# Projecting the scan outputs of two channel groups together in a state-space layer

## The chip, the cores and the metric

The kernel runs on one core of a Trainium2 chip. The metric is the device time of one execution in microseconds (us); lower is better. The core has a matrix engine (TensorE, PE in the profile; its weight loads are listed as PEld), three engines for element-wise work (VectorE or DVE, ScalarE or ACT, GpSimd or POOL) and a queue processor (SyncE or SP) that here only issues DMAs. Each engine takes its instructions in program order; engines meet through semaphores. On-chip data lie in SBUF, with 128 partitions (rows), and matrix products land in PSUM, which has eight banks of 128 x 512 float32.

## The reference

One layer of a convolutional network with a mixture of experts behind it, for 4 images of 256 channels and 32 x 32 = 1024 positions, in float32. The change concerns its first piece. The 256 normalised channels are split into 4 groups of 64 channels (NB = 4, DM = 64), and each group runs its own selective scan with 128 inner channels (DIN) and 16 states (DS):

```python
def selective_scan(u, dt, Bm, Cm, A, Dp):
    dA = jnp.exp(dt[..., None] * A)
    dBu = (dt * u)[..., None] * Bm[:, :, None, :]
    def step(h, inp):
        dA_t, dBu_t, C_t = inp
        h = dA_t * h + dBu_t
        return (h, jnp.einsum('bds,bs->bd', h, C_t))
    ...
    return ys.transpose(1, 0, 2) + u * Dp

def mamba(xs, inw, convw, convb, xpw, dtw, dtb, alog, dp, outw):
    xz = xs @ inw.T
    u, z = jnp.split(xz, 2, axis=-1)
    ...
    y = selective_scan(u, dt, Bm, Cm, -jnp.exp(alog), dp)
    return y * jax.nn.silu(z) @ outw.T
...
xc = xn.reshape(B, N, NB, DM).transpose(2, 0, 1, 3)
xm = mamba_v(xc, m_inw, m_convw, m_convb, m_xpw, m_dtw, m_dtb, m_alog, m_d, m_outw) + skip_scale * xc
```

The last factor of each group's output is the gate `silu(z)`, then comes the output projection from 128 inner channels to the group's 64 channels, and the normalised input scaled by `skip_scale` is added. Behind `xm` come one-dimensional convolutions, an eight-headed attention over the 1024 positions, a feed-forward product, a depthwise 3 x 3 convolution with normalisations, and at the end the experts (8 of them, two per position).

## The kernel before, in words

**Layout.** Channels lie on partitions, positions along the free axis. The 256 channels of an image are two blocks of 128 rows; `where(n)` gives for group n the block `c = n // 2` and its 64 rows `rows` within it. So groups 0 and 1 are the two halves of block 0, groups 2 and 3 those of block 1. Positions are treated in two halves h of 512 (HALF), one PSUM bank each.

**Parts and steps.** One image b, one group n and one half h make a part; `parts` lists all 32 of them, n before h, b outermost. A part has 16 scan steps. A step makes, for 32 inner channels and 4 states on 128 rows, the decay `exp(dt A)` on ACT (L718, `decay`, issued three steps ahead: LEAD = 3), the inflow `dt u B` on VectorE (L728), the scan itself on VectorE (L739) and the product with C on POOL (L747). TensorE spreads B over the rows (L710, `spread_b`) and sums the states into the PSUM tile `yp` (L757, `sums_of`).

**Order.** The whole stage is one hand-written order (`tc.manual_schedule`): `scan` (L833) emits, at each of the 16 steps, what the dictionaries `before`, `behind` and `group` name for that step. `before` finishes the previous part while the current one scans: at step 1 the last state sums, at step 3 `gather`, at step 6 `project_out`, at step 8 `add_skip`. So the output of part k is projected during part k+1. At the last part before an image's attention (the second half of group 1 in images 1 to 3), and at the very last part, `finish_part` (L868) does these things at once.

**The work that the change touches.** `gather` (L762) copies `yp` from PSUM to an SBUF tile `y` on ACT (L764) and multiplies it in place with the gate `z` on POOL (L765). `project_out` (L767) forms the group's output in a PSUM tile `op`: first the skip, a 64 x 64 diagonal product of the normalised input (L770), then the projection from 128 rows to the group's 64 rows added on top (L774). In float32 each of these matrix products shows as two records. `add_skip` (L776) copies the 64 rows on ACT into `XM[b]` (L780), the padded image that the convolutions read. `XM[b]` is taken from its pool when group 0's first half arrives. `z` is one tile for both halves of a group, filled by `copy_z` (L637) and passed through silu while the group before it scans.

**Beside the scan.** While image b scans, image b-1's later work is spread between its steps: `convolutions(b - 1)` from the start of image b, with diagonal products L426 and full 128 x 128 products L428 on TensorE, and after the fourth part the scan is halted for `attention(b - 1)` (L1117, L1137, L1163); then come `joined`, `local`, `around` and `sent_off`. `raw` (L1794) and its copy `XR` (L1786) lie in the last of these. What remains of image 3 and the experts comes after the last part.

**Buffers.** Tiles come from rotating pools: `act8` (8 buffers of 2 x 1024, where XM lies), `act4` (7 of 1024: z, u and others), `act2` (16 of 512: the decays, the scan outputs, y and others) and `psum` (8 banks, with op, yp, the B products and much of the work beside the scan). A tile whose buffer is still being read waits for that reader.

Of the kernel before, what the change touches and what calls it, by code (L numbers as in the profile page):

```python
# [9 lines left out]
F32 = mybir.dt.float32  # L10
AF = mybir.ActivationFunctionType
ALU = mybir.AluOpType
AX = mybir.AxisListType

P = 128
# [3 lines left out]
N = HH * WW  # L19
HALF = 512  # L20
NB, DM, DIN, DS, DTR, KC = 4, 64, 128, 16, 4, 4
# [3 lines left out]
LEFT = KC - 1  # L25
# [50 lines left out]
def network(  # L76
# [27 lines left out]
    nc = tc.nc  # L104
# [18 lines left out]
    def col(name, i=0, rows=slice(0, P)):  # L123
        at = _AT[name] + i
        return V[rows, at : at + 1]

    ident = cpool.tile([P, P], F32, name="ident")
# [19 lines left out]

    with tc.tile_pool(name="w_conv", bufs=1) as wp, tc.tile_pool(
        name="act8", bufs=8
    ) as act8, tc.tile_pool(name="act4", bufs=7) as act4, tc.tile_pool(  # L150
        name="act2", bufs=16
    ) as act2, tc.tile_pool(name="steps", bufs=2) as actd, tc.tile_pool(
        name="steps4", bufs=6
    ) as acts, tc.tile_pool(name="rows", bufs=3) as actc, tc.tile_pool(
        name="small", bufs=1
    ) as small, tc.tile_pool(
        name="spread", bufs=4, space=bass.MemoryType.DRAM
    ) as spread:

        XN = {}  # L160
# [10 lines left out]
        def load(ap, name, eng=None):  # L171
            t = wp.tile(list(ap.shape), F32, name=name)
            if eng is None:
                later.append((t, ap))
            else:
                eng.dma_start(t, ap)
            return t
# [10 lines left out]
        moutT_s = load(moutT, "moutT_s", nc.gpsimd)  # L188
# [135 lines left out]
        nc.vector.tensor_reduce(quads, ident.rearrange("p (s g) -> p g s", s=4), AX.X, ALU.add)  # L324
        A = wp.tile([P, GD, NB, GS], F32, name="A")
        inwk = wp.tile([P, NB, 2, DIN], F32, name="inwk")
        skips = wp.tile([P, DM], F32, name="skips")
        keeps = wp.tile([P, NB, P], F32, name="keeps")
        wdt = wp.tile([P, NB, DIN], F32, name="wdt")
        al = act4.tile([P, GD, NB * DS], F32, tag="a4", name="al")  # L330
# [6 lines left out]
        def weights():  # L337


            for n in range(NB):  # L340
                diag = a2(f"diag_{n}").rearrange("p (k d) -> p k d", k=KC)
                at = _AT["convw"] + n * KC
                nc.vector.tensor_tensor(
                    diag, ident.rearrange("p (a d) -> p a d", a=1).to_broadcast([P, KC, P]),
                    V[:, at : at + KC].rearrange("p (k a) -> p k a", a=1).to_broadcast([P, KC, P]),
                    ALU.mult,
                )
                taps = ps(f"taps_{n}")
                nc.tensor.matmul(
                    taps, ones, diag.rearrange("p k d -> p (k d)"), start=True, stop=True  # L350
                )
                yield 1
                for i in range(2):
                    r = ts(i, DM)
                    nc.vector.tensor_tensor(
                        inwk[r, n], taps[r].rearrange("p (k d) -> p k d", k=KC)[:, ts(i, 2), :],
                        inuT_s[r, n].rearrange("p (a d) -> p a d", a=1).to_broadcast([DM, 2, DIN]),
                        ALU.mult,
                    )

            for n in range(NB):
                xp = ps(f"xpw_{n}")
                nc.tensor.transpose(xp[0:DTR, 0:P], xpwT_s[:, n, 0:DTR], ident)
                xpw = a2(f"xpw_s_{n}", DTR)
                nc.scalar.copy(xpw[:, 0:P], xp[0:DTR, 0:P])
                yield 1
                wd = ps(f"wd_{n}")
                nc.tensor.matmul(wd[:, 0:P], xpw[:, 0:P], dtw_s[:, n, :], start=True, stop=True)
                nc.scalar.copy(wdt[:, n, :], wd[:, 0:P])
            for i, r in enumerate(states):  # L370
                nc.scalar.activation(
                    A[r].rearrange("p g n s -> p (g n s)"),
                    al[r].rearrange("p g c -> p (g c)")
                    .rearrange("p (x s) -> p x s", s=4)[:, :, i : i + 1]
                    .rearrange("p x s -> p (x s)"),
                    AF.Exp,
                )
            yield 1
            nc.vector.tensor_scalar(A, A, -1.0, None, ALU.mult)
            nc.vector.tensor_reduce(  # L380
                skips, ident.rearrange("p (s g) -> p g s", s=2), AX.X, ALU.add
            )
            nc.vector.tensor_scalar(skips, skips, col("skip"), None, ALU.mult)
            for n in range(NB):
                nc.vector.tensor_scalar(keeps[:, n, :], ident, col("dskip", n), None, ALU.mult)

        def ps(name):

            return psum.tile([P, HALF], F32, tag="ps", name=name)
# [4 lines left out]
        def a8_padded(name):  # L394
            t = act8.tile([P, NC2, N + 2], F32, tag="a8", name=name)
            nc.gpsimd.memset(t[:, :, 0:1], 0.0)
            nc.gpsimd.memset(t[:, :, N + 1 : N + 2], 0.0)
            return t

        def a4(name):  # L400
            return act4.tile([P, N], F32, tag="a4", name=name)

        def a2(name, rows=P):
            return act2.tile([rows, HALF], F32, tag="a2", name=name)

        def half(h):
            return ts(h, HALF)
# [81 lines left out]
        XM = {}  # L489
# [105 lines left out]
        T = {}  # L595
# [3 lines left out]
        def where(n):  # L599
            return n // 2, slice((n % 2) * DM, (n % 2) * DM + DM)  # L600
# [159 lines left out]
                )  # L760

        def gather(b, n, h):  # L762
            y = T[b, n, h, "y"] = a2(f"y_{b}_{n}_{h}")
            nc.scalar.copy(y, T[b, n, h, "yp"])  # L764
            nc.gpsimd.tensor_tensor(y, y, T[b, n, "z"][:, half(h)], ALU.mult)  # L765

        def project_out(b, n, h):  # L767
            c, rows = where(n)
            op = T[b, n, h, "op"] = ps(f"op_{b}_{n}_{h}")
            nc.tensor.matmul(  # L770
                op[rows], skips[rows], XN[b][rows, c, ds(LEFT + h * HALF, HALF)],
                start=True, stop=False,
            )
            nc.tensor.matmul(op[rows], moutT_s[:, n, :], T[b, n, h, "y"], start=False, stop=True)  # L774

        def add_skip(b, n, h):  # L776
            c, rows = where(n)
            if n == 0 and h == 0:
                XM[b] = a8_padded(f"xm_{b}")
            nc.scalar.copy(XM[b][rows, c, ds(1 + h * HALF, HALF)], T[b, n, h, "op"][rows])  # L780


        before = {
            1: [(sums_of, GS - 1)], 3: [(gather,)], 6: [(project_out,)], 8: [(add_skip,)],
        }

# [240 lines left out]

        def largest(b, g, q, k):

            each = small.tile([P, 4, N // P, 2], F32, tag="each", name=f"each_{b}_{g}")  # L1030
            for i in range(4):
                r = ts(i, HD)
                for qt in range(N // P):
                    for h in range(2):
                        sp = ps(f"sp_{b}_{g}_{i}_{qt}_{h}")
                        nc.tensor.matmul(
                            sp, q[r, ts(qt, P)], k[r, half(h)], start=True, stop=True
                        )
                        nc.vector.tensor_reduce(
                            each[:, i, qt, h : h + 1], sp, AX.X, ALU.max, negate=True  # L1040
                        )
            mneg = small.tile([P, 4 * N // P, 1], F32, tag="mneg", name=f"mneg_{b}_{g}")
            nc.vector.tensor_reduce(
                mneg, each.rearrange("p i t h -> p (i t) h"), AX.X, ALU.min
            )
            tp = ps(f"mT_{b}_{g}")
            nc.tensor.transpose(tp[0 : 4 * N // P, 0:P], mneg.rearrange("p i a -> p (i a)"), ident)
            mT = small.tile([4 * N // P, P], F32, tag="mT", name=f"mT_{b}_{g}")
            nc.scalar.copy(mT, tp[0 : 4 * N // P, 0:P])
            rows = a4(f"mrow_{b}_{g}")  # L1050
            for i in range(4):
                nc.sync.dma_start(
                    rows[HD * i : HD * i + 1, :].rearrange("a (t x) -> a t x", x=P),
                    mT[ts(i, N // P), :],
                )
            return rows
# [41 lines left out]
        def attention(b):  # L1098
# [4 lines left out]
            v8, qk = QKV.pop(b)  # L1103
            rows = [
                largest(b, g, qk[g][:, 0, :], qk[g][:, 1, :]) if shifted else None
                for g in range(2)
            ]
# [426 lines left out]
        with tc.manual_schedule(engines=ALL):  # L1534
            log_exp()
            start(weights(), first_normalised())
            drain()
            first_part()
            for b in range(B):
                for p in range(PARTS):  # L1540
                    at = b * PARTS + p
                    stop = b > 0 and p == PARTS // 2 - 1 or at == len(parts) - 1
# [72 lines left out]
class Experts:  # L1615
# [11 lines left out]
    T = 256  # L1627
# [798 lines left out]
```

## Time and profile before

| What | us |
|---|---|
| Three executions | 2192.04, 2197.09, 2203.86 |
| Median | 2197.09 |
| The profiled execution | 2216.93 |
| Its span, first to last instruction | 2215.0 |
| TensorE busy in it | 1975.0 |
| VectorE busy | 1534.4 |
| ACT busy | 1222.4 |
| POOL busy | 1047.5 |
| Mean granted TensorE clock | 0.947 of full speed |

All shares and instants are from the profiled execution. Its timeline falls into stages: image 0's scan alone until about 297 us; then, for each of images 1 to 3, four parts of scan with the convolutions of the image before (the last of these parts ends at about 440, 800 and 1202 us), that image's attention (until 536, 897 and 1298 us), and four more parts of scan. The last scan part ends at about 1460 us, and the rest of image 3 and the experts fill the time to 2215.

In the lines of the profile an instruction is named by its line in the kernel, its engine, its operation and its tiles (output <- inputs) with partitions x elements. A number in square brackets at the end of a timeline line is the time its engine stood idle before it, with what ended that.

### The profile page before, as it was taken

Reading aid. Unit: us, or ns where it says so; the run is one execution under the profiler, and the core shown is the slowest. Engines: PE = TensorE matmul, PEld = TensorE weight load, DVE = VectorE, ACT = ScalarE, POOL = GpSimd, SP = SyncE. Lnnn points to the kernel's source line nnn. Section 1 sums busy time; section 2 is a strip of 40 time slices with the busy share of each in tenths; the row PEclk is TensorE's granted clock in tenths of the full one; section 3 lists DMA queues with packets and bytes.
Section 4 is the critical chain, followed back from the end, with each engine's and each line's share of the span. In section 5 each row is a group of like instructions: output and inputs, shape, how many; then the busy total and the mean of one; then the engine's idle time right before and its main releaser. Section 6 shows DMA issues by size and latency. Waiting matters only on the chain. (4 is left out here: it accounts for less than half of the span.)

```text
span 2215.0 us, 28220 instructions
## 1 busy us (share of the span) xinstructions
PE 1975.0 (89%) x8722; PEld 879.7 (40%) x8722; DVE 1534.4 (69%) x2232; ACT 1222.4 (55%) x2288; POOL 1047.5 (47%) x930
## 2 busy tenths in 40 slices
PE   6878879999987999986889999678999989999995
PEld 2113112322212332322223223135732668888884
DVE  3999999858999978799798978984255355211211
ACT  4665657678767667675656765543248433222221
POOL 0787888612788740576975025741130012422221
PEclk8898999999999999998999999889989999999997
DMA  3664553401544421244533034353320166966665
GB/s 95 151 165 118 125 133 83 114 9 59 123 116 105 106 49 39 59 117 104 160 94 92 1 91 106 86 178 113 101 89 1 46 193 175 271 176 187 178 167 164
DMA packets 157088, 251.41 MB, mean 114 GB/s; under 512 B 34740, under 2 KB 101332, under 8 KB 156664
## 3 DMA queue, kind: packets, MB, share of 16 engines
q1 hardware_dynamic: 136560, 223.47, 36.3%
q0 software_dynamic: 12720, 17.32, 3.9%
q10 hardware_dynamic: 7640, 8.65, 1.2%
q8 instruction: 72, 1.18, 0.2%
q14 instruction: 96, 0.79, 0.1%
HBM read 137.22 MB, written 36.62 MB: 78 GB/s over the span
## 5 line engine op out<-in xcount | busy, mean ns | idle before, releaser
L747 POOL TENSOR_TENSOR dA<-hs,cs 128x512 f32<-128x512 f32 x512 | 682.2, 1342 | 388.5 <-DVE hs L739 268.9
L718 ACT ACTIVATE dA<-dts,A 128x512 f32<-128x512 f32 x512 | 358.8, 718 | 143.5 <-DMA dts<-dt 72.4
L2293 POOL DMA_INDIRECT Y<-ys,dest x68 | 108.9, 1601 | 528.3 <-DVE ys L2285 521.2
L757 PE MATMUL yp<-dA,quads 128*32 128x512 f32 x1024 | 272.2, 632 | 71.2 <-POOL dA L747 60.9
L1127 ACT ACTIVATE e<-st 128x512 f32<-128x512 f32 x512 | 263.7, 604 | 111.3 <-PE st L1117 89.3
L728 DVE TENSOR_TENSOR dBu<-dts,bs 128x512 f32<-128x512 f32 x384 | 259.9, 678 | 56.6 <-PE bs L710 18.1
L2258 ACT ACTIVATE hs<-h,b 128x256 f32<-128x256 f32 (+1 forms) x256 | 110.2, 479 | 339.6 <-PE h L2253 224.1
L2266 PE MATMUL y<-w,hs 128*128 128x256 f32 (+1 forms) x1088 | 245.7, 385 | 1.9 <-ACT hs L2258 1.9
L739 DVE TENSOR_TENSOR_SCAN hs<-dA,last,dBu 128x512 f32<-128x512 f32 x192 | 243.6, 1269 | 4.4 <-PE yp L757 1.3
L2253 PE MATMUL h<-xT,w 128*128 128x256 f32 (+1 forms) x1024 | 238.6, 389 | 0.2 <-DVE xT L2216 0.2
L739 DVE TENSOR_TENSOR_SCAN hs<-dA,dBu 128x512 f32<-128x512 f32 x192 | 231.8, 1207 | 9.6 <-PE av L1137 6.5
L1173 DVE TENSOR_TENSOR e<-e,e 128x512 f32<-128x512 f32 x256 | 170.3, 726 | 90.2 <-ACT e L1127 40.3
L2266 PEld LDWEIGHTS y<-w,hs 128*128 128x128 f32 (+1 forms) x1088 | 199.0, 190 | 39.2 <-issue 8.9
L2253 PEld LDWEIGHTS h<-xT,w 128*128 128x128 f32 x1024 | 195.2, 192 | 44.4 <-issue 11.0
L2216 DVE COPY xT<-xp 128x512 f32<-128x512 f32 (+1 forms) x36 | 23.3, 646 | 243.7 <-PE xp L2212 243.4
L710 PE MATMUL bs<-u,xpwT_s 128*32 128x512 f32 x1024 | 160.8, 660 | 34.7 <-DVE hs L739 14.4
L1117 PE MATMUL st<-qk 32*128 32x512 f32 x1024 | 182.0, 645 | 7.0 <-ACT e L1127 3.0
L757 PEld LDWEIGHTS yp<-dA,quads 128*32 128x32 f32 x1024 | 49.3, 113 | 270.1 <-POOL dA L747 169.6
L1163 PE MATMUL av<-e,v 128*32 128x512 f32 x1024 | 141.9, 618 | 0.0
L1117 PEld LDWEIGHTS st<-qk 32*128 32x128 f32 x1024 | 61.5, 184 | 126.3 <-issue 91.4
L1137 PE MATMUL av<-e,every 128*32 128x512 f32 x512 | 90.3, 623 | 3.1 <-DVE e L1173 3.0
L728 DVE TENSOR_TENSOR bs<-dts,bs 128x512 f32<-128x512 f32 x128 | 86.1, 673 | 1.3 <-DMA dts<-dt 1.3
(336 smaller groups left out, 2678.3 us busy)
## 6 DMA issues: line engine op xcount, KB each, us to landing
dts<-dt SPq DMA_DIRECT2D x512, 128.0 KB
w<-in_W_dram SPq DMA_DIRECT2D x124, 512.0 KB
cs<-cd SPq DMA_DIRECT2D x512, 64.0 KB
xs<-XS SPq DMA_DIRECT2D x32, 260.0 KB
xd<-xn SPq DMA_DIRECT2D x64, 128.0 KB
xn<-in_x_dram SPq DMA_DIRECT2D x8, 512.0 KB
XL<-xl SPq DMA_DIRECT2D x8, 512.0 KB
xl<-XL SPq DMA_DIRECT2D x4, 1024.0 KB
```

The source lines that it names most:

```text
L710: nc.tensor.matmul(bs[r], xpwT_s[:, n, s : s + 1].to_broadcast([P, 32]), T[b, n, "u"][:, half(h)], start=True, stop=True,)
L718: nc.scalar.activation(dA, T[b, n, h, "dts", g][:, 0, :], AF.Exp, scale=A[:, g, n, q : q + 1])
L728: nc.vector.tensor_tensor(dBu, T[b, n, h, "dts", g][:, 1, :], T[b, n, h, "bs", q], ALU.mult)
L739: nc.vector.tensor_tensor_scan(hs, T[b, n, h, "dA", i], dBu, 0.0 if h == 0 else last, ALU.mult, ALU.add)
L747: nc.gpsimd.tensor_tensor(dA, hs, T[b, n, h, "cs", q], ALU.mult)
L757: nc.tensor.matmul(T[b, n, h, "yp"][ts(g, 32)], quads, T[b, n, h, "dA", q * GD + g], start=False, stop=(q == GS - 1),)
L1117: nc.tensor.matmul(sts[i], k[r, ts(kt, P)], q[r, half(h)], start=True, stop=not shifted)
L1127: nc.scalar.activation(es[i], sts[i], AF.Exp, scale=1.0 / HD**0.5)
L1163: nc.tensor.matmul(accs[0][ts(i, HD)], v8[:, kt, ts(4 * g + i, HD)], es[i], start=(kt == 0), stop=(kt == NK - 1),)
L1173: nc.vector.tensor_tensor(first[i], first[i], es[i], ALU.add)
L2253: nc.tensor.matmul(hp[:, i, :], w1(c, k0 + i), xT[:, c, :], start=(c == 0), stop=(c == NC2 - 1))
L2266: nc.tensor.matmul(yp[ts(k % parts, n), ts(t % 2, C)], hidden(k)[:, ds(t * P, n)], w2(k), start=(k < parts), stop=(k >= NHC - parts),)
```

## The change

Groups 0 and 1 (and 2 and 3) share a block of 128 rows. The changed kernel leaves an even group's gated output where it is and projects it together with that of the odd group after it.

- `gather` writes the gated output into the gate's own tile `z`, and `y` is only read by that product.
- `project_out` and `add_skip` do nothing for even n. For odd n, `project_out` makes one skip product over all 128 rows of the block and then two projections, of the even group into rows 0 to 63 and of the odd one into rows 64 to 127 of the same PSUM tile; `add_skip` copies 128 rows.
- `XM[b]` is taken at group 1's first half, two parts later.
- `skips` becomes a 128 x 128 diagonal.
- The pool `act4` has eight buffers.
- Three small tiles in `largest`, which belongs to a second network that is not executed in these runs, are taken from `act2`.

```diff
-    ) as act8, tc.tile_pool(name="act4", bufs=7) as act4, tc.tile_pool(
+    ) as act8, tc.tile_pool(name="act4", bufs=8) as act4, tc.tile_pool(
...
-        skips = wp.tile([P, DM], F32, name="skips")
+        skips = wp.tile([P, P], F32, name="skips")
...
-            nc.vector.tensor_reduce(
-                skips, ident.rearrange("p (s g) -> p g s", s=2), AX.X, ALU.add
-            )
-            nc.vector.tensor_scalar(skips, skips, col("skip"), None, ALU.mult)
+            nc.vector.tensor_scalar(skips, ident, col("skip"), None, ALU.mult)
...
         def gather(b, n, h):
-            y = T[b, n, h, "y"] = a2(f"y_{b}_{n}_{h}")
+            y, z = a2(f"y_{b}_{n}_{h}"), T[b, n, "z"][:, half(h)]
             nc.scalar.copy(y, T[b, n, h, "yp"])
-            nc.gpsimd.tensor_tensor(y, y, T[b, n, "z"][:, half(h)], ALU.mult)
+            nc.gpsimd.tensor_tensor(z, y, z, ALU.mult)

         def project_out(b, n, h):
             c, rows = where(n)
-            op = T[b, n, h, "op"] = ps(f"op_{b}_{n}_{h}")
+            if n % 2 == 0:
+                return
+            op = T[b, c, h, "op"] = ps(f"op_{b}_{c}_{h}")
             nc.tensor.matmul(
-                op[rows], skips[rows], XN[b][rows, c, ds(LEFT + h * HALF, HALF)],
-                start=True, stop=False,
-            )
-            nc.tensor.matmul(op[rows], moutT_s[:, n, :], T[b, n, h, "y"], start=False, stop=True)
+                op, skips, XN[b][:, c, ds(LEFT + h * HALF, HALF)], start=True, stop=False
+            )
+            for i in range(2):
+                nc.tensor.matmul(
+                    op[ts(i, DM)], moutT_s[:, 2 * c + i, :],
+                    T[b, 2 * c + i, "z"][:, half(h)], start=False, stop=True,
+                )

         def add_skip(b, n, h):
             c, rows = where(n)
-            if n == 0 and h == 0:
+            if n % 2 == 0:
+                return
+            if n == 1 and h == 0:
                 XM[b] = a8_padded(f"xm_{b}")
-            nc.scalar.copy(XM[b][rows, c, ds(1 + h * HALF, HALF)], T[b, n, h, "op"][rows])
+            nc.scalar.copy(XM[b][:, c, ds(1 + h * HALF, HALF)], T[b, c, h, "op"])
...
-            each = small.tile([P, 4, N // P, 2], F32, tag="each", name=f"each_{b}_{g}")
+            each = a2(f"each_{b}_{g}")[:, 0 : 8 * N // P].rearrange(
+                "p (i t h) -> p i t h", i=4, h=2
+            )
...
-            mneg = small.tile([P, 4 * N // P, 1], F32, tag="mneg", name=f"mneg_{b}_{g}")
+            mneg = a2(f"mneg_{b}_{g}")[:, 0 : 4 * N // P].rearrange("p (i a) -> p i a", a=1)
...
-            mT = small.tile([4 * N // P, P], F32, tag="mT", name=f"mT_{b}_{g}")
+            mT = a2(f"mT_{b}_{g}", 4 * N // P)[:, 0:P]
```

## The prediction

> **What bounds the kernel now.** I read the busy times first, then the grouped instructions, the table by stage, the chain of waits and the timeline of TensorE and VectorE around single instructions of the change.
>
> ```profile
> PE 1975.0 (89%) x8722; PEld 879.7 (40%) x8722; DVE 1534.4 (69%) x2232; ACT 1222.4 (55%) x2288; POOL 1047.5 (47%) x930
> L774 PE MATMUL op<-y,moutT_s 128*64 128x512 f32 x64 | 36.1, 647 | 0.0
> L770 PE MATMUL op<-xn,skips 64*64 64x512 f32 x64 | 36.0, 644 | 0.0
> L780 ACT COPY xm<-op 64x512 f32<-64x512 f32 x32 | 18.6, 581 | 46.2 <-PE op L774 46.1
> ```
>
> TensorE (PE) is the busiest engine by far, but 89% is a mean over stages, so the table by stage decides (columns: window in us, its length, busy time with the number of instructions of PE, PEld, DVE, ACT and POOL, the granted clock, DMA share, GB/s).
>
> ```profile
> 374.00:536.00 162.00, 158.59 (x864) 51.00 (x866) 122.03 (x148) 119.23 (x228) 64.88 (x49) 0.98 0.22 60
> 536.00:695.00 159.00, 134.06 (x504) 34.03 (x504) 154.01 (x175) 112.54 (x207) 124.55 (x96) 0.99 0.48 119
> 770.00:897.00 127.00, 126.01 (x755) 38.75 (x755) 105.22 (x136) 91.05 (x178) 29.34 (x24) 1.00 0.16 42
> 1342.00:1386.00 44.00, 44.00 (x192) 18.26 (x192) 34.92 (x58) 21.94 (x38) 24.91 (x20) 0.97 0.38 102
> 1460.00:2215.00 755.00, 701.79 (x3318) 502.29 (x3318) 270.52 (x668) 259.60 (x504) 161.97 (x185) 0.96 0.50 145
> ```
>
> The kernel alternates. From about 381 to 536, 745 to 897, 1145 to 1298 and 1341 to 1386 us TensorE has no gap worth the name: there 1 us of TensorE is 1 us of the kernel. In the other scan stages, such as 536 to 695, VectorE is full (154.0 of 159) and TensorE has slack. The last 755 us hold no scan, so no instruction of the change except the last part's.
>
> ```profile
> 392.60 1.07 PE L770 MATMUL op<-xn,skips 64*64 64x512 f32 x2
> 393.60 1.07 PE L774 MATMUL op<-y,moutT_s 128*64 128x512 f32 x2
> 394.61 1.13 PE L426 MATMUL fp<-xl,ident 128*128 128x512 f32 x2
> 400.23 0.70 DVE L728 TENSOR_TENSOR dBu<-dts,bs 128x512 f32<-128x512 f32 x1 [4.82 <-PE bs L710]
> ```
>
> The first three lines give the price of one set: the skip starts at 392.60, the projection at 393.60, the next work at 394.61, so a set holds TensorE for 2.0 us. The records' mean of 644 ns counts overlapping pipeline and is not that price. The fourth shows that VectorE waited for TensorE 5 us later, so the set is on the path there.
>
> **What the Trainium skill says.** "TensorEngine Tiling (Array Packing)", Key Properties: different tiles load weights and multiply in parallel and are tied to partitions; in the 128x64 configuration there are two. The two projections of a pair (PSUM rows 0 to 63 and 64 to 127) are such tiles. Nothing here does it for this very line, but the half-width form exists:
>
> ```profile
> L2266 PE MATMUL y<-w,hs 128*64 128x256 f32 x64 | 7.8, 385 | 0.0
> L686 PE MATMUL cp<-u,xpwT_s 128*32 128x512 f32 x64 | 18.1, 608 | 0.0
> 399.09 1.06 PE L710 MATMUL bs<-u,xpwT_s 128*32 128x512 f32 x8
> ```
>
> 64 records of 385 ns side by side would be 24.6 us one after another; their union is 7.8, so they overlap about threefold. L710's eight quarter-width records of 512 columns end in 1.06 us, the time of two. The trace agrees with the page. "Perfetto Trace Analysis", Optimization Strategy, says that a kernel can have regimes with different most-contended engines; the table above shows exactly that, and it is why I sum by stage.
>
> **The change, part by part.** Each part (32 of them: image, group n, half) issues its set in the part after it. Before: 32 sets of 2.0 us. After: even n issues nothing; odd n issues one 128-row skip (two records of 512 columns, 1.0 us as any such pair) and two half-width projections beside each other (four records, taken at 1.0 us from L710). So odd sets stay at 2.0 us and the 16 even sets go: 32 us of TensorE, 32 records. ACT loses 16 copies (L780) of 581 ns, 9.3 us; a copy of 128 rows is taken as 0.58 us too, since L764 copies 128 rows in 574 ns. POOL's product only changes its output tile: 1327 ns as before. No DMA is added, removed or moved.
>
> What of the 32 us lies on the path? Numbering parts 0 to 31 (four images of eight), the even sets are those of parts 0, 1, 4 and 5 of each image:
> - Part 9 (set at 392.6), part 17 (752.5), part 25 (1154.5): TensorE runs on without a wait from there to the end of that image's attention, with VectorE waiting for it (4.82 us at 400.23, 1.63 at 760.16): 2.0 us each, 6.0.
> - Part 28 (1358.4): TensorE is 44.0 of 44 busy, and VectorE waits 3.19 us at 1361.73: 2.0.
> - Part 16 (its set lies just ahead of 734): VectorE waits 0.63 us for the product L710 there, which comes 2.0 us earlier: 0.6.
> - Part 21 (1000): VectorE stalls 1.41 us behind an ACT copy whose PSUM bank turns over with these tiles; afterwards POOL is the bound. Between 0 and 2.0; I take 0.7.
> - Parts 8 and 24 (350.7 and 1142): TensorE soon waits again for VectorE (2.10 us at 381.49, 2.09 at 1145.01), so the 2.0 us are swallowed: 0.
> - Parts 0, 1, 4, 5, 12, 13, 20, 29: VectorE or POOL is full around them, TensorE's 2.0 us are hidden: 0. If that cover were gone they would give up to 16 us in all.
>
> ```profile
> 381.49 1.22 PE L428 MATMUL fp<-d4r,fpwT_s 128*128 128x512 f32 x2 [2.10 <-DVE d4r L462]
> 760.16 0.70 DVE L728 TENSOR_TENSOR dBu<-dts,bs 128x512 f32<-128x512 f32 x1 [1.63 <-PE bs L710]
> 1361.73 0.70 DVE L728 TENSOR_TENSOR dBu<-dts,bs 128x512 f32<-128x512 f32 x1 [3.19 <-ACT XR L1786]
> ```
>
> Sum: 6.0 + 2.0 + 0.6 + 0.7 = 9.3 us.
>
> The odd set's projection waits for the odd part's POOL product, as it did; its even partner was ready two parts earlier. The merged skip needs all 128 rows of the normalised image, there for long. The new lifetime is that of the gated z of an even group: it is read until the odd group's projection, two parts (some 70 us) longer. act4 gets its eighth buffer for that; following each tile's slot in program order with the times of before, I find no tile of act4, act8, PSUM or the step pools that waits longer. In act2, where y is now free after POOL's product, two tiles would come later (an exp by 2.3 us around 159, covered by its lead of three steps of about 2.3 us; a scan output by 1.0 us at 1066, whose neighbour loses a wait of 3.0). The image's XM is taken two parts later, its edge memsets move with it on POOL (well under 1 us). Setup does one VectorE operation fewer. `largest` belongs to a fallback network that isn't executed. All at 0; bounds -3 to +3 us together.
>
> Against the profiled execution: 2216.9 (span 2215.0) becomes 2207.6. That execution lay 0.9% above the median; the saving is counted in the same microseconds, so 2197.1 becomes 2187.8; I say 2187.5.
>
> **Rivals.**
> A. The two projections do not run beside each other: they write one PSUM bank, in accumulation over what the skip left, which L2266 doesn't show. Then an odd set costs 3.0 us. In the stretches where TensorE binds there are two odd sets for each of three images (parts 10, 11, 18, 19, 26, 27): 6 us back, 2197.1 - 9.3 + 6 = 2193.8. Against: L757's four quarter-width tiles accumulate into one bank too, and eight of its records took 1.04 us at 399.98.
> B. More is on the path than I count. ACT sat idle 46.1 us before L780, waiting for L774 with exps and copies behind it, up to 7.0 us at once; half of these instructions go. If a third of those 46 us/2 reaches VectorE, 8 us come on top: 2180. Waits that speak for it: 3.19 us at 1361.73, of which I count 2.0, and the swallowed sets. Against: ACT is 55% busy and leads by three steps.
> C. Nothing moves: the freed TensorE time becomes waits for VectorE (69% on average, full in half the scan stages) and attention's own chain: 2197.
> D. Slower: z held longer makes ACT's copy into a new group's z wait for the pair's projection. It stands in ACT's in-order queue ahead of the exps, and the scan runs dry once the wait is over the lead of three steps, 6.9 us. At a wait of 12 us, four times one image each, the loss is 4 x 5.1 = 20 us, which against 9.3 is +11, the point where it decides; at 15 us it is 4 x 8.1 - 9.3 = +23: 2220. For it: ACT already waits for act2 slots (34.5 us in 28 waits of L718 for POOL). Against: the eighth buffer pays for just this tile.
>
> **How the numbers follow.** Forecast 50%, A 12%, B 18%, C 10%, D 10%. About 0.5% (11 us) is what a measurement here can tell from no change, and the three times shown scatter by 12. The forecast is 0.42% faster, so somewhat under half of it (20 points of 50) lands beyond 0.5%, B nearly wholly (17), A and C with 4: faster 0.41. Slower: D 0.09 and 0.01 of C. The rest, 0.49, is no change. The range runs from just below B (2176) to above C with its scatter (2202).
>
> **What would show it.** In the changed kernel: 32 records of L770's skip at 128x128, 64 of the projection, in pairs starting a few ns apart (right) or 0.5 us apart (A); odd sets of 2.0 us against 3.0; the attention stages that end at 536, 897 and 1298 now ending 2.0, 4.6 and 7.3 us earlier; the wait at 400 shrunk from 4.82 to about 2.8; ACT's wait for the projection about halved from 46.1. Wrong would be a new wait of ACT on its copy into z or of VectorE on an a2 slot, or scan stages of unchanged bounds that lengthen.

## The result

| | Median, us | Runs | Lowest to highest |
|---|---|---|---|
| Before | 2198.60 | 6 | 2192.04 to 2203.86 |
| Changed | 2182.47 | 6 | 2180.85 to 2183.93 |

The ratio is 0.9933, with a 95% interval of 0.9917 to 0.9950: about 16 us of median, at or beyond the 0.5% that the prediction took as what can be told from no change. In a later set of runs the same two kernels stood at 2214.91 and 2203.57 us, a ratio of 0.9944 (0.9926 to 0.9962): 11 us. Both points are larger than the 0.42% forecast; the second interval still holds 0.9958, the ratio of the forecast, the first does not. Four of the variants below have one execution far above the others (2273 to 3592 us) at another granted clock; it is in none of the figures.

The first part of the page of the changed kernel, and its groups of the instructions concerned (line, engine, operation and tiles, count, then busy time and mean ns of one, then idle time before them and what ended most of it):

```profile
PE 1937.3 (89%) x8690; PEld 874.4 (40%) x8690; DVE 1533.4 (70%) x2231; ACT 1212.4 (56%) x2272; POOL 1048.1 (48%) x930
L769 PE MATMUL op<-xn,skips 128*128 128x512 f32 x32 | 18.5, 663 | 0.0
L773 PE MATMUL op<-z,moutT_s 128*64 128x512 f32 x64 | 18.2, 647 | 0.0
L784 ACT COPY xm<-op 128x512 f32<-128x512 f32 x16 | 9.5, 592 | 10.6 <-PE op L773 10.6
```

TensorE's records fall from 8722 to 8690, and its busy time by 37.7 us, of which 12.7 lie in the last stretch (701.8 against 689.1), where the change has no part. The skip group's busy time halves (36.0 to 18.5), since half of the records are gone. The projection's halves too (36.1 to 18.2), although all 64 records are still there with the same mean of 647 ns: the two of a pair run beside each other. One copy now takes 592 ns for 128 rows where it took 581 for 64. ACT's idle time before it falls from 46.2 to 10.6 us.

One odd set, that of part 10, on the timeline of TensorE (start in us, duration, instruction):

```profile
418.59 1.02 PE L769 MATMUL op<-xn,skips 128*128 128x512 f32 x2
419.54 1.08 PE L773 MATMUL op<-z,moutT_s 128*64 128x512 f32 x4
420.55 1.99 PE L425 MATMUL qkp<-xl,wqkT_s 128*128 128x512 f32 x4
```

Four projection records end within 1.08 us. The next work starts 1.96 us after the skip: an odd set costs what one group's set cost before, for two groups.

What that frees shows in VectorE's wait for B, at the instruction that stood at 400.23 us with a wait of 4.82 in the profile of before:

```profile
394.66 1.06 PE L707 MATMUL bs<-u,xpwT_s 128*32 128x512 f32 x8
395.80 0.70 DVE L725 TENSOR_TENSOR dBu<-dts,bs 128x512 f32<-128x512 f32 x1 [2.76 <-PE bs L707]
```

The wait is 2.06 us shorter, which is the one set that went from TensorE's queue ahead of it.

And the table by stage, for the windows that correspond to those of before (window, its length, busy time with instructions of PE, PEld, DVE, ACT, POOL, granted clock, DMA share, GB/s):

```profile
532.00:689.00 157.00, 128.25 (x498) 32.57 (x494) 153.01 (x172) 109.63 (x203) 123.44 (x95) 1.00 0.49 120
765.00:891.00 126.00, 125.01 (x755) 38.38 (x755) 104.29 (x135) 89.82 (x175) 29.00 (x25) 1.00 0.16 41
1447.00:2180.00 733.00, 689.10 (x3320) 500.33 (x3320) 269.72 (x667) 259.80 (x504) 161.49 (x184) 0.97 0.52 149
```

The regimes are those of before: VectorE full in the first, TensorE in the second. The third line holds a trap: this last stretch is some 20 us shorter than that of before, and the next section shows that this is not the change's doing.

### The profile page after: what moved, and what is told of

Same layout as the page of the kernel before. It is cut to its first block, busy times and chain, and to the rows that moved or that the text cites. A ratio compares the mean times of both kernels' runs of the same rounds, so it can differ in the third digit from the quotient of the medians.

```text
span 2180.3 us, 28168 instructions
## 1 busy us (share of the span) xinstructions
PE 1937.3 (89%) x8690; PEld 874.4 (40%) x8690; DVE 1533.4 (70%) x2231; ACT 1212.4 (56%) x2272; POOL 1048.1 (48%) x930
## 5 line engine op out<-in xcount | busy, mean ns | idle before, releaser
L754 PE MATMUL yp<-dA,quads 128*32 128x512 f32 x1024 | 290.0, 640 | 85.3 <-POOL dA L744 74.0
L1123 PE MATMUL st<-qk 32*128 32x512 f32 x1024 | 174.8, 638 | 1.9 <-DVE hs L736 1.9
```

Of the source, the lines that this page charges most:

```text
L754: nc.tensor.matmul(T[b, n, h, "yp"][ts(g, 32)], quads, T[b, n, h, "dA", q * GD + g], start=False, stop=(q == GS - 1),)
L1123: nc.tensor.matmul(sts[i], k[r, ts(kt, P)], q[r, half(h)], start=True, stop=not shifted)
```

## The experiments

Ratios are to the kernel before, run on the same chip in the same set of runs; "the changed kernel" is the one described above.

**The kernel before, unchanged.** No edit.

> The kernel before, unchanged, for a second profile and for the scatter: 1.000 of before, within 0.003. In the profiles, the changed kernel gained 15 us up to the end of the last scan and 19 us after it, where nothing was changed. If the 19 us are the scatter of the profiled execution of before (which lay 0.9% above its median), this profile's stretch from the last scan part's start to the end is near 768 us, as in the changed kernel; if the change really shortens it, it is near 787.

Measured: 1.0002 (0.9989 to 1.0016), 2214.02 us. Its last stretch is as long as in the first profile of before, which seems to say that the change shortens it. But the changed kernel, profiled again beside its ACT variant below, and a variant of it with all TensorE work given back (the second such run), settle it. Last stretches of these three, in that order, each in the columns of the table by stage:

```profile
1461.00:2218.10 757.10, 701.78 (x3322) 501.15 (x3322) 274.38 (x672) 259.88 (x504) 165.05 (x191) 0.96 0.49 145
```

```profile
1448.30:2205.70 757.40, 699.31 (x3324) 502.12 (x3324) 274.76 (x673) 259.40 (x504) 165.85 (x191) 0.96 0.50 145
```

```profile
1450.00:2187.60 737.60, 690.17 (x3320) 500.21 (x3320) 270.96 (x669) 259.77 (x504) 162.92 (x187) 0.96 0.51 149
```

These windows begin up to 4.7 us before the last scan ends. Counted from that end, the stretch takes 752.5 to 757.1 us in nine of the fourteen profiles, those of before among them, and 734.5 to 737.4 in five, the first one of the changed kernel among them. The changed kernel is in both groups, so the change does not make the difference; it goes with the set of runs. Most of it lies in one place, the attention of image 3, here from its first score product (`st`) to its last product with the values (`av`) in the same three profiles:

```profile
1622.00:1724.20 102.20, 99.43 (x642) 28.14 (x641) 53.72 (x90) 69.92 (x137) 21.27 (x35) 0.93 0.12 38
1613.40:1712.40 99.00, 93.28 (x642) 26.99 (x641) 53.77 (x90) 69.61 (x137) 21.83 (x35) 0.95 0.13 39
1611.30:1697.80 86.50, 86.50 (x642) 24.65 (x641) 53.71 (x90) 69.49 (x137) 21.85 (x35) 1.00 0.15 45
```

The same 642 records take 99 to 102 us at a granted clock of 0.93 to 0.95 in the long group and 86.5 at 1.00 in the short one. What lowers the clock there in some sets of runs, and whether the lower clock or a stall comes first, stays open. Chip number 6 had a set of each kind, so the number does not tell them apart. Where the stretch is long, the median of before is 2213 to 2215 us, where it is short 2197 to 2199. The first profile of before (2216.93 us) is of the long kind although the executions timed for it are not, and the first one of the changed kernel is of the short kind; so these two may only be compared up to the last scan.

Over that range I averaged the lengths of groups of parts in three profiles of before (with the run of eight buffers below) and four of the changed kernel (with its two ACT variants below). A part is counted from the start of its first scan instruction, the last one to the end of its last:

| Stretch, by parts | Before, us (lowest to highest) | Changed | Difference | Forecast |
|---|---|---|---|---|
| before the first scan | 54.6 to 55.9 | 52.1 to 54.4 | -2.3 | 0 |
| 0 to 8 | 276.4 to 282.5 | 278.0 to 280.4 | -0.8 | 0 |
| 9 to 11, with an attention | 201.9 to 203.8 | 199.6 to 201.5 | -2.1 | -2.0 |
| 12 to 15 | 123.5 to 125.0 | 123.5 | -0.5 | 0 |
| 16 to 19, with an attention | 236.2 to 239.4 | 233.1 to 236.2 | -2.3 | -2.6 |
| 20 to 23 | 158.8 to 160.3 | 155.8 to 160.5 | -1.7 | -0.7 |
| 24 to 27, with an attention | 240.4 to 241.3 | 236.6 to 241.0 | -2.8 | -2.0 |
| 28 to 31 | 162.3 to 163.1 | 158.7 to 162.2 | -2.6 | -2.0 |

Parts 12 to 15, where VectorE is full, lose two sets and gain nothing: they take 123.5 us in every profile but the first of before. From part 9 on the sum is -11.9 us against -9.3 forecast. The spread of one stretch between profiles of one kernel is up to 6.1 us, so single rows say little. The first row is not the change's: the variants below, which set up as the changed kernel does, take 53.3 to 55.3 us there. And the sum is probably too large. The profiled executions of before and of its eight-buffer variant in one set of runs lay 6.0 and 4.1 us above the medians of their kernels, while the four of the changed kernel and its ACT variants lay at theirs on average.

**TensorE's work given back.** The even sets return, into a PSUM tile that nobody reads; all else stays changed.

```diff
             if n % 2 == 0:
+                idle = ps(f"idle_{b}_{n}_{h}")
+                nc.tensor.matmul(
+                    idle[rows], skips[rows, rows], XN[b][rows, c, ds(LEFT + h * HALF, HALF)],
+                    start=True, stop=False,
+                )
+                nc.tensor.matmul(
+                    idle[rows], moutT_s[:, n, :], T[b, n, "z"][:, half(h)], start=False, stop=True
+                )
                 return
```

> The changed kernel with TensorE's work given back: at each even group a 64x64 skip product and a 128x64 projection into a PSUM tile that nobody reads, where the kernel before had them; ACT's copies stay saved. Theory 1 (the gain is TensorE time in the stretches where TensorE binds, some 9 us of the 15): 9 us slower than the changed kernel, 0.997 of before. Theory 2 (the gain comes from ACT, which no longer waits for the product and copies): no slower than the changed kernel, 0.993 of before. If all of the gain is TensorE's: 1.000 of before.

Measured: 1.0013 (1.0003 to 1.0022). The gain is gone although ACT still saves 16 copies and its wait for the projection is as short as in the changed kernel. The groups show that TensorE's work came back in full and ACT's wait did not:

```profile
L772 PE MATMUL idle<-z,moutT_s 128*64 128x512 f32 x32 | 17.2, 618 | 0.0
L768 PE MATMUL idle<-xn,skips 64*64 64x512 f32 x32 | 17.1, 615 | 0.0
L792 ACT COPY xm<-op 128x512 f32<-128x512 f32 x16 | 9.4, 590 | 10.2 <-PE op L781 10.2
```

The edit also takes a PSUM tile for each even set, as the kernel before did. What that tile's turn costs was not separated from TensorE's time, here and in the other runs that give sets back.

**ACT's work given back**, twice, and the changed kernel beside the second.

```diff
             if n % 2 == 0:
+                nc.scalar.copy(T[b, n, "z"][0:DM, half(h)], T[b, n, "z"][0:DM, half(h)])
                 return
```

> The changed kernel with ACT's work given back: at each even group, where the kernel before copied 64 rows out of PSUM, ACT copies 64 rows of the gated output onto themselves; it waits for POOL's product, long done, and not for TensorE. Theory 1: as the changed kernel, 0.993 of before. Theory 2 (ACT's busy time matters): 9.3 us of copies come back, part of them on the path, 0.995 to 0.997 of before.

> The changed kernel, unchanged, beside its variants on one chip. On an earlier chip it stood at 0.9933 of before; the variant with ACT's copies given back stood at 0.9961, on another. If ACT's copies cost nothing, this run stands where that one stood, 0.996, and the chips differ; if they cost what the two numbers say, it stands at 0.993.

> The changed kernel with 64-row copies of the even groups' gated outputs on ACT given back, again, beside the changed kernel itself. Theory 1 (only TensorE's time counts): equal to the changed kernel within 0.15%. Theory 2 (ACT's 9.3 us are on the path in part): 0.2 to 0.4% slower than it.

Measured: 0.9961 (0.9946 to 0.9975) alone; then, side by side, 0.9944 (0.9926 to 0.9962) for the changed kernel and 0.9944 (0.9926 to 0.9962) with the copies. In the profile of the second one they are there, 9.8 us of busy time:

```profile
L781 ACT COPY z<-z 64x512 f32<-64x512 f32 x16 | 9.8, 614 | 0.0
```

Side by side the medians differ by under 2 us, so ACT's 16 copies cost nothing that can be measured here. Nor are the 36 us that ACT no longer waits for the projection a gain in themselves: the variant before this one kept that short wait and lost the gain.

**Eight buffers alone**, on the kernel before: `act4` with `bufs=8`, and the three tiles of `largest` moved to `act2` as in the change.

> The kernel before with act4 at eight buffers alone (the three small tiles of the fallback network moved to act2 to make room, as the change does). Theory 1: nothing, 1.000 of before within 0.002, since no act4 tile waits in the trace of before. Theory 3 (the eighth buffer brings part of the gain): 0.996 to 0.998 of before.

Measured: 0.9999 (0.9987 to 1.0011). The eighth buffer brings nothing by itself. It was added to make room for the gated output that lives longer; whether the merge needs it was not tried on the chip.

**Which sets count.** The second experiment's edit, at some parts only (for the other eleven, `in` stands for `not in`):

```diff
+            if n % 2 == 0 and 2 * NB * b + 2 * n + h not in {9, 16, 17, 25, 28}:
+                return
             if n % 2 == 0:
+                idle = ps(f"idle_{b}_{n}_{h}")
...
```

> TensorE's skip and projection given back at five of the sixteen even sets only: parts 9, 16, 17, 25 and 28, where the prediction put 8.6 of its 9.3 us. If the places are right, this loses nearly all that giving back all sixteen loses, 8 to 10 us against the changed kernel (0.4%); if the gain is spread evenly, five sixteenths of it, 3 to 5 us (0.2%).

> The other eleven even sets given back: parts 0, 1, 4, 5, 8, 12, 13, 20, 21, 24 and 29. If the places are right, at most 1 to 2 us slower than the changed kernel (part 21, 0.1%); if the gain is spread evenly, eleven sixteenths of it, 8 to 10 us (0.4%); if sets that I put at nothing matter (8, 24, 29), something between.

Measured in the same set of runs as the changed kernel's 0.9944: 0.9978 (0.9962 to 0.9995) with the five given back, 0.9946 (0.9925 to 0.9966) with the other eleven. In medians that is +5.8 and +0.2 us; by the ratios 0.34% and 0.02%, or 7.5 and 0.4 us of 2215. Ten microseconds of TensorE at five places undo most of the gain, and twenty-two at the eleven others change nothing that can be seen. The interval of the five touches that of the changed kernel at its end, so the size is known to a few microseconds only. The profiles agree: from the first scan of part 9 to the end of the last scan they show 1121.2 us with the five and 1111.3 with the eleven, where before takes 1124.8 to 1128.5 and the changed kernel 1109.4 to 1118.4.

**Whether neighbours add up.** Giving back all sixteen had cost more than five and eleven together, so the neighbours 8, 24 and 29 were added to the five, and all sixteen were run again.

> TensorE's work given back at the five sets of before and at their neighbours: parts 8, 9, 16, 17, 24, 25, 28 and 29. All sixteen cost 1.0013 against 0.9944, more than the five (0.9978) and the other eleven (0.9946) together. If sets in neighbouring parts add up (what the one leaves behind, the other finds on the path), this stands at 1.000 to 1.001; if the sum of the parts holds and the rest was scatter, at 0.998.

> All sixteen even sets of TensorE given back, once more. The first time this stood at 1.0013 of before, though the five (0.9978), the eight (0.9984) and the eleven (0.9946, as the changed kernel) leave only about 0.998 for it. If that was scatter between chips, it stands at 0.997 to 0.999 now; if sets beside sets cost more than their sum, at 1.001 again.

Measured: 0.9984 (0.9973 to 0.9995) for the eight, and 0.9982 (0.9971 to 0.9993) for all sixteen, where the same kernel had stood at 1.0013. The two results for all sixteen differ by 0.3% and their intervals do not overlap, so ratios from two sets of runs can differ by more than their intervals say; effects below that are told apart only within one set. The eight and the five were in different sets, so that the eight cost no more is likely, but not shown: no sign was found that neighbours add up.

**The pair not packed.** At each odd set the old form runs for both groups, one after the other.

```diff
-            nc.tensor.matmul(
-                op, skips, XN[b][:, c, ds(LEFT + h * HALF, HALF)], start=True, stop=False
-            )
             for i in range(2):
+                r = ts(i, DM)
+                nc.tensor.matmul(
+                    op[r], skips[r, r], XN[b][r, c, ds(LEFT + h * HALF, HALF)],
+                    start=True, stop=False,
+                )
                 nc.tensor.matmul(
-                    op[ts(i, DM)], moutT_s[:, 2 * c + i, :],
+                    op[r], moutT_s[:, 2 * c + i, :],
                     T[b, 2 * c + i, "z"][:, half(h)], start=False, stop=True,
                 )
```

> The changed kernel with the pair not packed: at each odd set a 64x64 skip and a projection for each of the two groups, one after the other, 4.0 us of TensorE instead of 2.0; ACT's copies stay merged. Six odd sets lie where TensorE binds (parts 10, 11, 18, 19, 26, 27), 12 us there: 0.9944 + 0.0054 = 1.000 of before. If the time on TensorE at an odd set didn't matter, 0.994; if every odd set counted, 32 us, 1.009.

Measured: 1.0021 (1.0011 to 1.0032), slower than before although TensorE does exactly the work of before. Its timeline and the stage of the first attention, then the same stage in the changed kernel:

```profile
421.13 1.07 PE L771 MATMUL op<-xn,skips 64*64 64x512 f32 x2
422.13 1.07 PE L775 MATMUL op<-z,moutT_s 128*64 128x512 f32 x2
423.13 1.07 PE L771 MATMUL op<-xn,skips 64*64 64x512 f32 x2
424.13 1.07 PE L775 MATMUL op<-z,moutT_s 128*64 128x512 f32 x2
425.13 5.42 PE L425 MATMUL qkp<-xl,wqkT_s 128*128 128x512 f32 x12
```

```profile
408.50:538.10 129.60, 129.60 (x769) 40.69 (x769) 91.48 (x114) 96.31 (x185) 38.23 (x31) 1.00 0.16 48
```

```profile
406.10:531.60 125.50, 125.50 (x765) 40.27 (x765) 91.43 (x115) 96.29 (x184) 38.25 (x31) 1.00 0.18 49
```

The set takes 4.0 us instead of 2.0, and the stage with two such sets is 4.1 us longer: TensorE is busy in all of it. Merging without packing gives up what the change saves: sets that cost little where they were, such as those of parts 8 and 24, move to where they cost all they take. Over the three images this stage takes 129.6, 130.8 and 129.8 us against 125.5, 126.7 and 124.6 in a profile of the changed kernel, some 13 us in all. By the ratios the whole lies 17 to 19 us above the changed kernel, but across sets of runs. Against before, in the same set, it is 2 to 7 us, and 13 less the forecast's 9.3 is 3.7.

**The skip on VectorE** in the six odd sets that TensorE's stretches hold.

```diff
-            nc.tensor.matmul(
-                op, skips, XN[b][:, c, ds(LEFT + h * HALF, HALF)], start=True, stop=False
-            )
+            lone = b > 0 and c == 0
+            if not lone:
+                nc.tensor.matmul(
+                    op, skips, XN[b][:, c, ds(LEFT + h * HALF, HALF)], start=True, stop=False
+                )
...
-                    T[b, 2 * c + i, "z"][:, half(h)], start=False, stop=True,
+                    T[b, 2 * c + i, "z"][:, half(h)], start=lone, stop=True,
...
+            if b > 0 and c == 0:
+                nc.vector.scalar_tensor_tensor(
+                    XM[b][:, c, ds(1 + h * HALF, HALF)], XN[b][:, c, ds(LEFT + h * HALF, HALF)],
+                    col("skip"), T[b, c, h, "op"], ALU.mult, ALU.add,
+                )
+                return
```

> The changed kernel with the skip of the six odd sets in TensorE's stretches taken from it: for groups 0 and 1 of images 1 to 3 there is no skip product, and VectorE makes XM as input times scale plus projection (one operation of 128x512), in place of ACT's copy. If TensorE's time is what counts there and VectorE has room, six times 1.0 us: 0.9944 - 0.0027 = 0.992 of before. If VectorE's extra operation (about 0.7 us) waits for the projection and holds back the scan, 0.994 or more.

Measured: 0.9908 (0.9886 to 0.9929), 2176.86 us against 2196.75. It is the fastest here, though not in the same set of runs as the changed kernel, whose interval it overlaps. Its stage of the first attention and its new instruction:

```profile
408.30:531.90 123.60, 123.60 (x761) 39.56 (x761) 92.75 (x116) 95.22 (x183) 38.24 (x31) 1.00 0.17 49
```

```profile
L787 DVE SCALAR_TENSOR_TENSOR xm<-xn,V,op 128x512 f32<-128x512 f32 x6 | 4.4, 734 | 0.0
```

The stage is 1.9 us shorter than in the changed kernel, for two skip products of 1.0 us. VectorE never sat idle before its six new operations, and is busy 92.8 of the 123.6 us: it had the room. The six copies of ACT that fall away with them are of the kind that cost nothing above.

## Why the prediction was right, and where it may have been too small

- **The bound.** TensorE in some stretches, VectorE in the others: shown by the five sets that cost 7.5 us and the eleven that cost 0.4. The prediction had 8.6 and 0.7 at these places. The end of each attention, forecast 2.0, 4.6 and 7.3 us earlier, came 5.3, 8.0 and 12.5 us earlier in the averages; 3.1 of these stand before part 9 already, where no gain was forecast and scatter is the likely reason.
- **The odd set at 2.0 us.** Shown: 1.96 us at 418.59. Rival A (no packing) is out, and the unpacked variant shows what it would have been.
- **ACT's 9.3 us at nothing.** Shown: 0.9944 with and without the copies in one set; the earlier 0.9961 overlaps it. Rival B, that ACT's wait hides a further gain, finds no support. The wait went from 46 to 11 us, much further than the prediction's "about halved", and with TensorE's work given back it stayed at 10 us without a gain to match.
- **Buffers at nothing.** Shown for the eighth buffer alone. Rival D's long wait did not appear: ACT sat idle 3.8 us in all before its copies into `z` in the changed kernel, and waited for the product that they copy, not for the projection.
- **Rival C,** nothing moves: out by both intervals.
- **The size.** The forecast was 9.3 us; the medians show 16 in one set and 11 in the other. Only the first interval excludes the forecast, and by less than the 0.3% by which two sets differed for one kernel, so that 9.3 us were too few is likely and not shown. The forecast's chances put faster by over 0.5% at 0.41, a little under no change. By the averages the shortfall from part 9 on is in no row over 1.0 us, which is scatter as likely as gain. All sixteen sets given back left 0.18% in one set of runs and cost 0.13% more than before in another, and their profiles show 1121.4 and 1115.6 us from part 9 to the last scan, between before and the changed kernel. So these runs do not tell whether anything beyond TensorE's time gives a part of the gain.
- **The Trainium skill** said, in "TensorEngine Tiling (Array Packing)", Key Properties, that different tiles multiply in parallel; here four records of a pair took 1.08 us, where two took 1.07 before, with both tiles adding to what the full-width skip had left in the same PSUM tile. The threefold overlap that the prediction read from L2266 is not packing alone: the full-width records of that line, 1024 of 385 ns in 238.2 us, overlap 1.7-fold one after another.

## What to carry to other kernels

Price a saving by the stage it falls in: here ten microseconds of TensorE at five places were worth more than twenty-two at eleven others. Merging work of two groups paid here when the merged work was packed, and cost when it was only postponed into a stage where that engine is full; a small product in such a stage could go to an engine with room. And before comparing two profiles, compare a stretch that the change doesn't touch: 20 us of difference here were not the change's, and the granted clock of that stretch, stage by stage, showed where they lay.

## What the runs showed of the hardware

The stretch after the last scan took 752.5 to 757.1 us in some sets of runs and 734.5 to 737.4 in others. In the windows shown TensorE was busy 699 to 702 us of it against 689 to 690. The changed kernel was profiled in both kinds, before only in the long one; medians of before lay at 2213 to 2215 and at 2197 to 2199 us accordingly. In the three profiles shown, 12.5 to 15.7 us of the difference are one dip of the granted clock in the attention of image 3, to 0.93 to 0.95 on average over 99 to 102 us, where the other kind ran 86.5 us at 1.00. In the second profile of the changed kernel it was down to 0.50 from 1638 to 1643 us; TensorE had stood idle for the 5.7 us before, and the profile shows nothing that it waited for.

In the changed kernel, a full-width float32 skip product of two records holds TensorE for 0.95 us at 418.59, where its neighbour before it was full-width too, and a projection of two half-width tiles beside each other for 1.01 us.
